# Four edits to a one-core adapter kernel: b2 of four batches by VectorE, a second W1 copy loaded four batches sooner, a ninth W1 by id, and a last store in halves

## Chip, core and metric

The kernel runs on one core of a Trainium2 chip. The metric is the device time of one execution in microseconds (us). Before the change the median of three runs is 308.9 us (308.59 to 309.42). The profiled execution took 308.95 us; its trace spans 307.2 us, so 1.75 us lie outside the span, and the TensorE clock granted over the span was 0.989 (1.00 in every stage up to 300 us).

## What is computed

There are 128 batches `b`, each a matrix `x[b]` of 128 rows by 512 columns in fp32, and each with an id `v = itok[b]` that picks one of 10 adapters:

```python
h = relu(x[b] @ W1[v] + b1[v])          # 512 -> 128
y = x[b] + h @ W2[v] + b2[v]            # 128 -> 512
n = (y - mean(y)) * rsqrt(var(y) + 1e-5)
out[b] = x[b] + n * gamma[v] + beta[v]
```

## The kernel before, in words

One batch is one tile of 128 partitions by 512 columns. One pass of the main loop (from L515, `i` from 3 to 129) moves the pipeline on by one batch: TensorE (PE) transposes batch `i` (four 128x128 transposes, L234), multiplies batch `i-1` by W1 (`down`, L257) and batch `i-2` by W2 (`up`, L274). ScalarE (ACT) copies the transposed batch out of PSUM (`copy_xT`, L238), applies bias and relu (L265), copies the W1 of a coming batch out of a resident table (`stage_w1`, L225) and squares with a sum (L310). VectorE (DVE) works on batch `b = i-3` and on the pair before: residual with its sum (L291), mean, the steps of the reciprocal root (L324, L326, L329), scaling by gamma (L353) and the final multiply-add (`finish`, L362). GpSimd (POOL) adds beta to x for every batch (L251) and b2 to x for most (L244). SyncE (SP) issues nearly all DMAs. Each engine's order is written by hand: `keep` ties each instruction behind the one before it on its engine, so an instruction that waits holds back everything behind it.

**b2** comes by one of three ways: POOL adds it to x ahead of time (`add_b2`); or PE adds it by a matmul of a one-column selector with the table rows, 96x512 in bf16, ahead of the W2 matmul (`b2_by_matmul`, L273); or DVE adds a row of the spread table `b2_b` to the result in PSUM (`vector_b2`, L284).

**W1** reaches a batch by three ways. Batches 0 to 7 get theirs from HBM by id (`load_first`, L154, 256 KB each, into a pool of five `w1s` buffers). From batch 8 on ACT copies it from a resident table. There are two tables: `w1e`, with rows grouped so that each partition holds four neighbouring rows of W1 (`load_early`, two DMAs of 1280 KB), for batches below EARLY = 24, whose transposes then read every fourth column of x; and `w1`, in the regular order, loaded in four quarters of 640 KB in runs of 512 bytes (`load_w1`, L103), for batches from 24 on. A quarter is a range of the reduction, not of the ids, so the first copy out of `w1` needs all four. FIRST = 8 is the first batch with a copy by ACT.

**SP's queue** around the change, in order: after the early loads come x of batches 12 to 15; the store of batches 0 and 1; x of 16 to 19; the stores of 2 and 3 and of 4 and 5; quarter 0 of `w1`; x of 20 to 23; the store of 6 and 7; quarter 1; the store of 8 and 9; quarter 2; x of 24 to 27; the store of 10 and 11; quarter 3. Each store (512 KB, L366) waits on SP for the DVE's `finish` of its second batch.

In ACT's order of pass `i` stand `copy_xT(i)`, `relu(i-1)`, `stage_w1(i+1)` and `square(i-3)`, from pass 11 on; PE has one PSUM buffer for the transposes, so those of batch `i+1` wait until `copy_xT(i)` has emptied it.

At the end (`tail`) the last five batches are finished one by one; the last one is scaled and finished over all 512 columns (L419) and stored by one DMA from SP (L415).

Of the kernel before, what the change touches and what calls it, by code (L numbers as in the profile page):

```python
# [16 lines left out]
P = 128  # L17
G = 4
EPS = 1e-5
FIRST = 8  # L20
EARLY = 24
LATE = 12
U = 2

# [2 lines left out]
def cond_resid_kernel(ctx: ExitStack, tc: tile.TileContext, x, itok, W1, b1, W2, b2, gamma, beta, out):  # L27
# [8 lines left out]
    nc = tc.nc  # L36
    B, S, H = x.shape
# [8 lines left out]
    def keep(ins):  # L46

        engine = ins.ins.engine
        if engine in last:
            tc.add_manual_dep(ins.ins, last[engine], behind, reason="kept order")  # L50
        last[engine] = ins.ins.name
        return ins
# [14 lines left out]
    E = B - 5  # L67
# [6 lines left out]
    def xb(b):  # L74
        return xs[b // G][:, b % G, :]
# [11 lines left out]
    def load_part(lo, hi):  # L87
        dst = xs[lo // G][:, lo % G : lo % G + hi - lo, :]
        keep(nc.sync.dma_start(out=dst, in_=x[lo:hi].rearrange("b s h -> s b h")))
# [11 lines left out]
    def load_w1(k):  # L101
        keep(
            nc.sync.dma_start(out=w1[:, :, k, :], in_=W1[:, k * P : (k + 1) * P, :].rearrange("l p a -> p l a"))  # L103
        )
# [28 lines left out]
    def lid(b, engine):  # L133
        g = b // G
        if (g, engine) not in lids:
            loads, vals = nc.values_load_multi_w_load_instructions(
                lang[0:1, g * G : (g + 1) * G],
                engines=[engine],
                min_val=0,
                max_val=L - 1,  # L140
                skip_runtime_bounds_check_because="clamped on the chip to 0..L-1 above",
            )
            for ins in loads:
                keep(ins)
            lids[g, engine] = vals
        return lids[g, engine][b % G]
# [4 lines left out]
    def load_first(b):  # L151
        w1s[b] = wp.tile([P, KC, A], FP, tag="w1s", name=f"w1s_{b}")
        src = W1[bass.ds(lid(b, ET.SP), 1)].rearrange("o (p k) a -> p (o k a)", k=KC)
        keep(nc.sync.dma_start(out=w1s[b].rearrange("p k a -> p (k a)"), in_=src))  # L154
# [5 lines left out]
    def load_early(lo, hi):  # L160
        dst = w1e[:, lo:hi].rearrange("p l k a -> p l (k a)")
        keep(nc.sync.dma_start(out=dst, in_=W1[lo:hi].rearrange("l (p k) a -> p l (k a)", k=KC)))
# [13 lines left out]
    xs[2] = xp.tile([P, G, H], FP, tag="x", name="x_2")  # L176
    load_part(2 * G, 2 * G + 2)
    load_early(0, 5)
    load_early(5, L)
    load_part(2 * G + 2, 3 * G)  # L180

    left = rp.tile([P, H], FP, tag="r", name="left")
# [29 lines left out]
    xT, hT, rs, os, ys, ssqs, nmeans, rstds = {}, {}, {}, {}, {}, {}, {}, {}  # L212
# [1 line left out]


    def b2_by_matmul(b):
        return b in (0, 1, 2, 3, 5, B - 1) or (b % 32 == 30 and b < E)

    def b2_by_vector(b):
        return 8 <= b < B - 8 and (b % 4 == 1 if b < 24 else b % 16 in (1, 6, 11))  # L220

    def stage_w1(b):
        w1s[b] = wp.tile([P, KC, A], FP, tag="w1s", name=f"w1s_{b}")
        src = (w1e if b < EARLY else w1).rearrange("p l k a -> p (l k a)")[:, bass.ds(lid(b, ET.Activation) * (KC * A), KC * A)]
        keep(nc.scalar.copy(w1s[b].rearrange("p k a -> p (k a)"), src))  # L225

    def transpose_x(b):
        pxs[b] = p_x.tile([P, KC, P], FP, tag="xT", name=f"pxT_{b}")
        for k in range(KC):
            if b < EARLY:  # L230
                cols = xb(b).rearrange("s (p k) -> s k p", k=KC)[:, k, :]
# [54 lines left out]
    def residual(b):  # L286
        r = rs.pop(b) if b in rs else xb(b)
        if b % 2 == 0:
            sums[b // 2] = st.tile([P, 2], FP, tag="sum", name=f"sum_{b // 2}")
        keep(  # L290
            nc.vector.scalar_tensor_tensor(ys[b], ys[b], 1.0, r, ALU.mult, ALU.add, accum_out=col(sums, b))  # L291
        )
# [45 lines left out]
    def deviation(g):  # L338
        root(ssqs[g], of_pair(g)[0])

    def rstd(g, n):
        t, u = of_pair(g)
        if n < 3:
            newton(n, ssqs[g], t, u)
        else:
            rstds[g] = st.tile([P, 2], FP, tag="rstd", name=f"rstd_{g}")
            newton_3(rstds[g], t, u)
            del ssqs[g], parts_of[g]
# [20 lines left out]
    def on(b):  # L369
        return 0 <= b < B  # L370
# [26 lines left out]
    def rstd_col(b):  # L397
        return rstds[b] if b > E else rstds[b // 2][:, b % 2 : b % 2 + 1]
# [12 lines left out]
        o = os[b // 2][:, b % 2, cols]  # L411
        keep(nc.gpsimd.tensor_tensor(o, n, o, ALU.add))

    def store_last(b, engine=nc.sync):
        keep(engine.dma_start(out=out[b], in_=os[b // 2][:, b % 2, :]))  # L415

    def finish_cols(b, cols=slice(0, H)):
        o = os[b // 2][:, b % 2, cols]
        keep(nc.vector.scalar_tensor_tensor(o, ys[b][:, cols], rstd_col(b), o, ALU.mult, ALU.add))  # L419

    def tail(b):
        p = E // 2
        residual(b)
        if b == E + 1:
            rstd(p, 1)
            scale(E - 1)
            rstd(p, 2)
            finish(E - 2)
            store(p - 1)
            rstd(p, 3)  # L430
            deviation_of(b)
            shift(E)
            by_pool(E, False)
        elif b == E + 2:
            rstd_of(b - 1, 1)
            negative_means(b // 2)
            rstd_of(b - 1, 2)
            finish_cols(E - 1)
            store_last(E - 1)
            rstd_of(b - 1, 3)  # L440
            store_last(E)
            deviation_of(b)
        elif b == E + 3:
            left, right = slice(0, H // 2), slice(H // 2, H)
            shift(b - 2)
            by_pool(b - 2, False)
            residual(b + 1)
            rstd_of(b - 1, 1)
            scale(b - 1)
            negative_means(b // 2)  # L450
            rstd_of(b - 1, 2)
            deviation_of(b)
            scale(b)
            rstd_of(b - 1, 3)
            rstd_of(b, 1)
            deviation_of(b + 1)
            rstd_of(b, 2)
            finish_cols(b - 1, right)
            by_pool(b - 1, True, left)
            store_last(b - 2, nc.scalar)  # L460
            store_last(b - 1, nc.scalar)
            rstd_of(b, 3)
            rstd_of(b + 1, 1)
            finish_cols(b)
            store_last(b)
            rstd_of(b + 1, 2)
            scale(b + 1)
            rstd_of(b + 1, 3)
            finish_cols(b + 1)
            store_last(b + 1)  # L470


    def spin(n, width):
# [41 lines left out]
    for i in range(3, B + U):  # L515
        b = i - U - 1
        if b > G and b % G == 2 and b // G + 3 < NG:
            load_x(b // G + 3)
        if i == 5:
            load_x(3)  # L520
        if i in (12, 14, 16, 18):
            load_w1((i - 12) // 2)
        if i == 4:
            up(2)
        if i == 5:
            up(3)
        if i > 3 and on(i):
            transpose_x(i)
        if b <= E:
            add_b2(b + 2)  # L530
            add_beta(b)
        if i > 4 and on(i - 1):
            down(i - 1)
        if i > 3 and on(i):
            copy_xT(i)
        if i > 4 and on(i - 1):
            relu(i - 1)
        if i + 1 >= LATE and on(i + 1):
            stage_w1(i + 1)
        if i > 5 and on(i - U):  # L540
            up(i - U)


        g, half = divmod(b, 2)
        p = g - 1
        mine, old = 0 <= p < B // 2, 0 <= p - 1 < B // 2
        if b == E:
            add_b2(b + 3)
            add_beta(b + 1)
            add_b2(b + 4)  # L550
            for n in range(b + 2, B):
                add_beta(n)
        if b > E:
            tail(b)
        elif half == 0:
            if on(b):
                vector_b2(b)
                residual(b)
            if mine:
                scale(2 * p)  # L560
                rstd(p, 1)
            if old:
                finish(2 * p - 1)
                store(p - 1)
        else:
            if on(b):
                vector_b2(b)
            if mine:
                rstd(p, 2)
            if on(b):  # L570
                residual(b)
            if mine:
                rstd(p, 3)
                scale(2 * p + 1)
            if on(b):
                negative_means(g)
            if mine:
                finish(2 * p)
        if 0 <= b <= E:
            square(b)  # L580
            if half == 1:
                deviation(g)
        if FIRST <= i + 1 < LATE:
            stage_w1(i + 1)

        for n, engine in ((i + 3, ET.Activation), (i - U + 3, ET.PE), (b + 1, ET.DVE), (b + 5, ET.Pool)):
            if on(n):
                lid(n, engine)
# [37 lines left out]
```

## Time and profile before

| what | number |
|---|---|
| median of three runs | 308.9 us |
| profiled execution, its own time | 308.95 us |
| its span | 307.2 us |
| PE busy | 296.1 us (96%) |
| DVE busy | 294.7 us (96%) |
| POOL busy | 284.4 us (93%) |
| ACT busy | 280.5 us (91%) |
| DMA | 77.59 MB, mean 253 GB/s |

A busy share says how long an engine had work in it, with overlapping instructions counted once. The timeline lists instructions in order: start, length, engine, line, operation, out<-in, and in brackets the idle time before it with what ended it. The view of stages gives the busy time of each engine, the granted clock, the share of the 16 DMA engines and the GB/s. For a DMA the timeline shows only the time of issuing it; its transfer and its landing (the moment at which its completion is signalled) are later, and are read from the answer for its line and from the trace's records of packets and landings.

### The profile page before, as it was taken

What the parts mean: (1) busy time and instruction counts of PE and PEld (TensorE: products, weight loads), DVE (VectorE), ACT (ScalarE), POOL (GpSimd) and SP (SyncE); (2) the same over time, 40 slices, a digit from 0 to 9 for tenths busy, and PEclk for the clock granted to TensorE, in tenths of its full rate; (3) what the DMA queues carried; (4) which work ended last, traced back from release to release, by engine and by line L of the source; (5) the groups of instructions that cost most, each with busy time, mean ns of one, the idle gap of its engine ahead of it and who ended that gap; (6) DMA issues with size and microseconds to landing.
All of it is one profiled execution on the core that took longest, in us unless ns stands there. A gap on an engine that the chain in (4) does not pass through costs nothing. (4 is left out here: it accounts for less than half of the span.)

```text
span 307.2 us, 6980 instructions
## 1 busy us (share of the span) xinstructions
PE 296.1 (96%) x1841; PEld 220.6 (72%) x1841; DVE 294.7 (96%) x825; ACT 280.5 (91%) x716; POOL 284.4 (93%) x238
## 2 busy tenths in 40 slices
PE   8999999999999999999999999999999999999970
PEld 3757778777777777777777777777777777777740
DVE  6877999999999999999999999999999999999994
ACT  3858999999999999999999999999999999999982
POOL 1349999998999999999999999999999999999994
PEclk9999999999999999999999999999999999999995
DMA  6999969986777667767876676777767666782244
GB/s 233 390 389 385 384 221 369 358 300 229 247 274 265 219 205 227 254 230 247 274 265 211 195 234 247 249 248 274 237 222 235 223 237 221 276 273 109 110 160 171
DMA packets 43481, 77.59 MB, mean 253 GB/s; under 512 B 1929, under 2 KB 7060, under 8 KB 43442
## 3 DMA queue, kind: packets, MB, share of 16 engines
q1 hardware_dynamic: 43094, 76.57, 72.2%
q10 hardware_dynamic: 348, 0.57, 0.5%
q8 instruction: 15, 0.25, 0.3%
q14 instruction: 24, 0.20, 0.2%
HBM read 43.58 MB, written 33.55 MB: 251 GB/s over the span
## 5 line engine op out<-in xcount | busy, mean ns | idle before, releaser
L251 POOL TENSOR_TENSOR o<-x,beta_b 128x512 f32<-128x512 f32 x128 | 163.4, 1289 | 9.5 <-DVE beta_b L210 9.5
L257 PE MATMUL ph<-xT,w1s 128*128 128x128 f32 x1024 | 135.3, 275 | 0.0
L244 POOL TENSOR_TENSOR r<-x,b_b 128x512 f32<-128x512 f32 x97 | 125.0, 1289 | 8.5 <-DVE b_b L210 6.2
L274 PE MATMUL py<-w,hT 128*128 x256 | 131.2, 594 | 0.0
L257 PEld LDWEIGHTS ph<-xT,w1s 128*128 128x128 f32 x1024 | 124.9, 192 | 1.0 <-ACT hT L265 0.5
L234 PEld LDWEIGHTS pxT<-ident,x 128*128 128x128 f32 x512 | 66.5, 152 | 66.0 <-issue 32.1
L353 DVE SCALAR_TENSOR_TENSOR py<-py,nmean,gamma_b 128x512 f32<-128x512 f32 x126 | 95.0, 754 | 0.0
L310 ACT ACTIVATE sq<-py,sum 128x512 f32<-128x512 f32 x124 | 86.3, 696 | 5.4 <-DVE nmean L298 2.4
L362 DVE SCALAR_TENSOR_TENSOR o<-py,rstd,o 128x512 f32<-128x512 f32 x122 | 90.9, 745 | 0.0
L234 PE MATMUL pxT<-ident,x 128*128 128x128 f32 x512 | 78.5, 276 | 0.0
L238 ACT COPY xT<-pxT 128x512 f32<-128x512 f32 x128 | 74.7, 584 | 3.9 <-PE pxT L234 3.9
L291 DVE SCALAR_TENSOR_TENSOR py<-py,r 128x512 f32<-128x512 f32 x97 | 67.1, 692 | 1.4 <-PE py L274 1.2
L225 ACT COPY w1s<-w 128x512 f32 x104 | 64.1, 616 | 0.0
L265 ACT ACTIVATE hT<-ph,b1T 128x128 f32<-128x128 f32 x128 | 47.3, 370 | 4.9 <-PE ph L257 2.5
L274 PEld LDWEIGHTS py<-w,hT 128*128 128x128 f32 x256 | 39.4, 192 | 1.8 <-issue 0.9
L310 ACT ACTIVATION_READ_ACCUMULATOR sq<-py,sum 128x1 f32 x124 | 25.4, 205 | 0.0
L291 DVE SCALAR_TENSOR_TENSOR py<-py,x 128x512 f32<-128x512 f32 x31 | 21.6, 698 | 1.6 <-issue 0.8
L320 ACT ACTIVATE root<-ssq,eps 128x2 f32<-128x2 f32 x62 | 16.5, 265 | 2.1
L284 DVE TENSOR_TENSOR py<-py,b_b 128x512 f32<-128x512 f32 x22 | 15.2, 691 | 0.1
L291 DVE DVE_READ_ACCUMULATOR py<-py,r 128x1 f32 x97 | 13.8, 142 | 0.0
L225 ACT COPY w1s<-w1e 128x512 f32 x16 | 9.8, 611 | 1.1 <-DMA w1e<-in_L_cond_W_dram 1.1
L324 DVE SCALAR_TENSOR_TENSOR part<-ssq,root 128x2 f32<-128x2 f32 x62 | 9.4, 151 | 0.9 <-ACT root L320 0.8
(54 smaller groups left out, 96.1 us busy)
## 6 DMA issues: line engine op xcount, KB each, us to landing
out_dram<-o SPq DMA_DIRECT2D x61, 512.0 KB, 3.3
x<-in_x_dram SPq DMA_DIRECT2D x29, 1024.0 KB, 6.4
x<-in_x_dram SPq DMA_DIRECT2D x6, 512.0 KB, 8.9
w1e<-in_L_cond_W_dram SPq DMA_DIRECT2D x2, 1280.0 KB, 11.7
w<-in_L_cond_W_dram SPq DMA_DIRECT2D x4, 640.0 KB, 7.4
w1s<-in_L_cond_W_dram SPq DMA_DIRECT2D x8, 256.0 KB, 8.2
w<-in_L_cond_W_dram SPq DMA_DIRECT2D x1, 1792.0 KB, 10.1
out_dram<-o SPq DMA_DIRECT2D x4, 256.0 KB, 2.0
```

The costliest lines, as they stand in the source:

```text
L225: keep(nc.scalar.copy(w1s[b].rearrange("p k a -> p (k a)"), src))
L234: keep(nc.tensor.transpose(pxs[b][:, k, :], cols, ident))
L238: keep(nc.scalar.copy(xT[b], pxs.pop(b)))
L244: keep(nc.gpsimd.tensor_tensor(rs[b], xb(b), b2_b[:, bass.ds(v * H, H)], ALU.add))
L251: keep(nc.gpsimd.tensor_tensor(os[g][:, j, :], xb(b), beta_b[:, bass.ds(v * H, H)], ALU.add))
L257: nc.tensor.matmul(phs[b], lhsT=w1s[b][:, k, :], rhs=xT[b][:, k, :], start=(k == 0), stop=(k == KC - 1))
L265: keep(nc.scalar.activation(hT[b], phs.pop(b), AF.Relu, bias=b1T[:, bass.ds(lid(b, ET.Activation), 1)]))
L274: keep(nc.tensor.matmul(ys[b], lhsT=hT[b], rhs=w2[:, bass.ds(v * H, H)], start=not m, stop=True))
L291: nc.vector.scalar_tensor_tensor(ys[b], ys[b], 1.0, r, ALU.mult, ALU.add, accum_out=col(sums, b))
L310: nc.scalar.activation(sq, ys[b], AF.Square, bias=col(sums, b), scale=-float(H), accum_out=col(ssqs, b))
L353: nc.vector.scalar_tensor_tensor(ys[b], ys[b], col(nmeans, b), gamma_b[:, bass.ds(v * H, H)], ALU.add, ALU.mult)
L362: nc.vector.scalar_tensor_tensor(o, ys.pop(b), rstds[g][:, j : j + 1], o, ALU.mult, ALU.add)
```

## The change

Four edits:

1. `b2` of batches 0 to 3 moves from the selector matmul on PE to an add on DVE.
2. The four quarters of `w1` are issued in passes 8, 10, 12 and 14 instead of 12, 14, 16 and 18, and `w1` is used from batch 16 on instead of 24.
3. Batch 8 also gets its W1 by id. Its load stands between the two halves of `load_early`, and the copy of batch 8 by ACT goes.
4. The last batch is finished and stored in two halves of 256 columns: the left one is issued by SP, the right one by ACT.

```diff
-FIRST = 8
-EARLY = 24
+FIRST = 9
+EARLY = 16
...
     load_early(0, 5)
+    load_first(2 * G)
     load_early(5, L)
...
     def b2_by_matmul(b):
-        return b in (0, 1, 2, 3, 5, B - 1) or (b % 32 == 30 and b < E)
+        return b in (5, B - 1) or (b % 32 == 30 and b < E)
 
     def b2_by_vector(b):
-        return 8 <= b < B - 8 and (b % 4 == 1 if b < 24 else b % 16 in (1, 6, 11))
+        return b < 4 or 8 <= b < B - 8 and (b % 4 == 1 if b < 24 else b % 16 in (1, 6, 11))
...
-    def store_last(b, engine=nc.sync):
-        keep(engine.dma_start(out=out[b], in_=os[b // 2][:, b % 2, :]))
+    def store_last(b, engine=nc.sync, cols=slice(0, H)):
+        keep(engine.dma_start(out=out[b][:, cols], in_=os[b // 2][:, b % 2, cols]))
...
-            finish_cols(b + 1)
-            store_last(b + 1)
+            for cols, engine in ((left, nc.sync), (right, nc.scalar)):
+                finish_cols(b + 1, cols)
+                store_last(b + 1, engine, cols)
...
-        if i in (12, 14, 16, 18):
-            load_w1((i - 12) // 2)
+        if i in (8, 10, 12, 14):
+            load_w1((i - 8) // 2)
```

## Prediction

> **What bounds the kernel.** The chain of waits explains only 2% of the span, so I read the stages first, then each engine's timeline. From 40 to 290 us PE, DVE and POOL are all busy for 99.9% of each stage. Which one sets the pace is seen in PE's timeline (start, length):
>
> ```profile
> 48.15 0.63 PE L234 MATMUL pxT<-ident,x 128*128 128x128 f32 x4
> 48.61 1.06 PE L257 MATMUL ph<-xT,w1s 128*128 128x128 f32 x8
> 49.50 1.02 PE L274 MATMUL py<-w,hT 128*128 x2
> 50.37 0.63 PE L234 MATMUL pxT<-ident,x 128*128 128x128 f32 x4
> ```
>
> These are the transposes of batch 16, `down` of 15, `up` of 14 and the transposes of 17. They follow each other at 0.46, 0.89 and 0.87 us, 2.22 us a pass; from batch 24 on, with regular transposes, at 0.44, 0.89 and 0.86, 2.19 a pass. After 35 us no pass is longer, but for 0.22 where a selector matmul stands. DVE's residual starts 0.04 to 1.03 us after the end of its batch's `up`, at batch 127 0.04 us: DVE is as loaded, but never further behind. So a hole in PE's stream is not made up later: a us lost there is a us at the end.
>
> **ACT is the way in.** Its timeline, at the copy of batch 16 (the ninth L225, since the first, at 31.29, is batch 8's):
>
> ```profile
> 47.79 0.61 ACT L225 COPY w1s<-w1e 128x512 f32 x1
> 48.30 0.70 ACT L310 ACTIVATE sq<-py,sum 128x512 f32<-128x512 f32 x1
> 48.88 0.20 ACT L310 ACTIVATION_READ_ACCUMULATOR sq<-py,sum 128x1 f32 x1
> 48.97 0.59 ACT L238 COPY xT<-pxT 128x512 f32<-128x512 f32 x1
> ```
>
> Behind the copy stand the square of batch 12 and `copy_xT(16)`, for which PE's transposes of 17 wait (one PSUM buffer). After a late start of that copy, PE goes on 1.18 + 0.59 + 0.05 (hand-over, as at 32.40 to 32.45) = 1.8 us later. What such a wait looks like is there already once, on the first table:
>
> ```profile
> 31.29 0.62 ACT L225 COPY w1s<-w1e 128x512 f32 x1 [1.05 <-DMA w1e<-in_L_cond_W_dram]
> ```
>
> **The DMAs.** SP's issues, and the DMA share by stage (last two columns: share of the 16 engines, GB/s):
>
> ```profile
> 39.87 1.31 SPq L103 DMA_DIRECT2D w<-in_L_cond_W_dram  x1
> 41.28 0.76 SPq L71 DMA_DIRECT2D x<-in_x_dram  x1
> 44.39 0.38 SPq L366 DMA_DIRECT2D out_dram<-o  x1
> 44.83 0.46 SPq L103 DMA_DIRECT2D w<-in_L_cond_W_dram  x1
> ```
> ```profile
> 34.00:38.00 4.00, 4.00 (x26) 2.94 (x26) 3.58 (x12) 3.97 (x12) 4.00 (x4) 1.00 1.04 400
> 38.00:40.00 2.00, 2.00 (x15) 1.53 (x14) 1.94 (x6) 2.00 (x5) 2.00 (x2) 1.00 0.18 68
> 42.00:46.00 4.00, 4.00 (x26) 3.06 (x26) 4.00 (x13) 3.96 (x11) 4.00 (x4) 1.00 0.88 270
> 46.00:50.00 4.00, 4.00 (x29) 3.29 (x28) 4.00 (x12) 3.83 (x12) 4.00 (x5) 1.00 1.06 378
> ```
>
> The engines are full until the early loads have drained (38.2 us by the packet records), have a dip of 2 us, and are full again when the quarters of `w1` come. Before, the last quarter is issued at 53.76, lands at 62.7, and is first read at 65.6: 3 us to spare.
>
> ```profile
> DMA to landing us min/median/max: 6.3/7.4/8.9
> ```
>
> That is the answer for L103: three of the four quarters have a landing, and none took under 6.3 us.
>
> **Part 2, W1 sooner: the price.** Quarter 3 now stands behind the store of 6 and 7 in pass 14. That store was issued at 44.39; with about 1.1 us of gain at the start (below) it goes at 43.3, and quarter 3 at 43.7. Its reader, ACT's copy of batch 16 in pass 15, would come at 47.79 - 1.1 = 46.7. The lead has shrunk from 11.8 us to 3.0, under half the shortest landing. When does it land? I take the engines as serving SP's DMAs in order, as the landings of before suggest: x of 20 to 23, issued 1.4 us after quarter 0, landed at 47.8, after its 46.2; quarter 2 (55.3) ahead of x of 24 to 27 (57.4), issued right behind it. Bytes ahead: before, everything up to the store of 2 and 3 had drained at 38.2. Added are W1 of batch 8 (256 KB at 390 GB/s, 0.7) and quarters 0 and 1, which now come before that point. A quarter's packets of 512 bytes go at 284 GB/s (43 to 44 us, where nothing else moved), 2.3 us each. So 38.2 + 0.7 + 4.6 = 43.5 with no dip. Then the store of 4 and 5 (512 KB, 1.35), quarter 2 (2.3), x of 20 to 23 (1 MB, 2.7), the store of 6 and 7 (1.35) and quarter 3 (2.3): 53.5. From the last packet to the landing the four quarters took 0.8 to 1.7, mean 1.1: **54.6**. The copy of 16 waits 54.6 - 46.7 = 7.9 us on ACT; behind it the square, `copy_xT(16)`, then all of PE from the transposes of 17 on. Those come at 54.6 + 1.8 = 56.4 instead of 50.37: **+6.0**. Bounds for the landing: 50.0 if it takes the shortest landing of a quarter (43.7 + 6.3), 57.3 if it takes that of x of 12 to 15 in the storm of early loads, 13.6. That makes +1.4 and +8.7; I take 54.6, since the queue ahead is counted from bytes.
>
> The Trainium skill, "DMA: Bandwidth & Descriptors", section "Queues, rings and completion order", says that SP's DMAs share one row of rings, and that each engine consumes a ring in order: this speaks against the change, since a load issued sooner into a full queue doesn't overtake. The landings above agree. The same page's fit for one DMA, 2.0 us plus bytes over 436e3 (section "Anatomy of one DMA", made on GpSimd's path), would give an estimate of 3.5 us, a landing at 47.2 and the second rival's time below; no quarter here was that quick.
>
> Its gain: seven passes from batch 17 to 23 with regular transposes, 2.22 to 2.19: **-0.2**. Earlier ones lie before the wait.
>
> **Part 1, b2 on DVE.** PE loses four matmuls at 0.22 us (20.09 to 20.32):
>
> ```profile
> 20.09 0.38 PE L273 MATMUL py<-parts,pick 96*128 96x512 bf16 x1
> 20.32 1.02 PE L274 MATMUL py<-w,hT 128*128 x2
> ```
>
> -0.9 on PE up to batch 5. DVE gains four adds of 0.70 and 0.03 of hand-over (48.41 to 49.13 at L284), 2.9 us, and between 19.5 and 27.91 it has 0.84 + 0.33 + 0.82 + 0.85 = 2.8 us idle: they fill it, and the residual of batch 4 stays at 27.9. Without that idle time they would cost up to 2.9. From there DVE runs at its own 2.07 a batch (a pair from 42.28 to 46.42) instead of at PE's, and reaches batch 8 at 36.2 instead of 37.31: -1.1 on both engines.
>
> **Part 3, a ninth W1 by id.** Its buffer is free when `down(3)` ends (17.0); SP gets there at 16.6, so SP waits 0.4 and has a register load and 0.4 of issue, and behind it stand the second half of `w1e` and x of 10 and 11, all in a queue ten us long: they land 0.7 later, `w1e` at 31.9, x of 10 at 33.3. ACT no longer needs `w1e` at 30.2 but at about 32.5, so its 1.05 us wait goes, and with it 0.15 + 0.11 + 0.04 in PE's passes of 9 to 11: -0.3. POOL, idle 0.69 for x of 10 now, idles 1.4, and leads DVE by 4 us or more all the way: nothing.
>
> All of parts 1 and 3 comes before 50 us, and the wait of part 2 ends by bytes, not by when ACT arrives: it swallows them. **0.**
>
> **Part 4, halves.** A half costs DVE 0.40 to its successor (300.42 to 300.82 at L419), so the left store leaves 0.3 sooner, the right ends 0.1 later and has ACT's issue (0.38) behind that of batch 125 (to 303.6). But from 303 to 305.5 the DMA engines are full with the four last stores: their bytes end when they ended. 0, within -0.3 and +0.3.
>
> **Sum**, against the execution's own 308.95 (the median, 308.9, is as good as equal): +6.0 - 0.2 + 0 = **314.8**. Bounds: +1.4 - 0.2 gives 310.2, +8.7 - 0.2 gives 317.5.
>
> **Rivals.** (a) *The queue is shorter than its bytes* (DMAs overtake, or the dip is used better): the landing is at 50.0 to 52, time 310.2 to 312.2. For it: the 6.3 us of quarter 0. Against: that one was issued into the dip, which is gone. (b) *No wait*: quarter 3 lands by 47.4, where 47.4 + 1.8 meets PE's transposes of 17 at 50.37 - 1.1 = 49.2; from there on parts 1 and 3 count. DVE's 1.1 is the smaller gain and sets it: 307.8. For it: only that SP issues the quarter 3 us ahead. Against: a landing of 3.7 us, where 6.3 is the least seen. (c) *The move of the quarters does not take effect*: each stays behind a store's wait for DVE; but these waits are of passes 7, 9, 11 and 13, so the issues do come 9 us sooner, at 30.0, 34.2, 38.8 and 43.7. It falls.
>
> **Chances**: forecast (312.3 to 317.5) 0.77; (a) 0.12; above 317.5 0.03; within 0.3% (what a measurement of this kernel can tell from no change) 0.02; (b) 0.06. So slower 0.92, same 0.02, faster 0.06; the range 310.2 to 317.5 holds 0.89.
>
> **What would show it.** On ACT, one idle stretch of some 8 us ahead of the first copy out of `w1`, ended by a DMA, near 46.7 to 54.6; one hole of 6 to 7 us in PE before the transposes of 17; the DMA share near 1 from 38 to 54 with no dip; before the hole, `up(4)` 0.9 sooner, the residual of 4 at 27.9, no wait at the copy of batch 9; after it 2.19 a pass. Wrong if the hole is missing (then rival b, and my reading of the queue falls), or if ACT waits at batch 9 too.

## The result and the profile after

The changed kernel takes 316.5 us (median of six runs, 315.97 to 317.83) against 309.15 us before. The ratio, an estimate from all runs and not the quotient of the two medians, is 1.0246 with a 95% interval of 1.0224 to 1.0267. The profiled execution took 316.37 us, with a span of 314.6 us: 7.4 us more than the one before. The forecast was 314.8 us, in a range of 310.2 to 317.5.

ACT's timeline of the kernel after, at the copies of batches 15 and 16:

```profile
44.41 0.61 ACT L226 COPY w1s<-w1e 128x512 f32 x1
...
46.41 0.37 ACT L266 ACTIVATE hT<-ph,b1T 128x128 f32<-128x128 f32 x1
54.30 0.62 ACT L226 COPY w1s<-w 128x512 f32 x1 [7.52 <-DMA w<-in_L_cond_W_dram]
54.83 0.68 ACT L311 ACTIVATE sq<-py,sum 128x512 f32<-128x512 f32 x1
55.41 0.19 ACT L311 ACTIVATION_READ_ACCUMULATOR sq<-py,sum 128x1 f32 x1
55.50 0.57 ACT L239 COPY xT<-pxT 128x512 f32<-128x512 f32 x1
```

The first copy out of `w1` waits 7.52 us for a DMA; it had been ready at 46.8. The square and the copy of the transposed batch 16 stand behind it, as the prediction said. What PE's timeline of the kernel after shows at this place:

```profile
47.03 0.60 PE L235 MATMUL pxT<-ident,x 128*128 128x128 f32 x4
47.46 1.06 PE L258 MATMUL ph<-xT,w1s 128*128 128x128 f32 x8
48.36 1.02 PE L275 MATMUL py<-w,hT 128*128 x2
56.13 1.11 PE L235 MATMUL pxT<-ident,x 128*128 128x128 f32 x4 [6.75 <-ACT xT L239]
57.03 1.92 PE L258 MATMUL ph<-xT,w1s 128*128 128x128 f32 x8
58.74 1.53 PE L275 MATMUL py<-w,hT 128*128 x2
60.10 0.60 PE L235 MATMUL pxT<-ident,x 128*128 128x128 f32 x4
```

The hole is where it was forecast: the transposes of batch 17 come at 56.13 instead of 50.37. But look at the pass behind the hole. `down` takes 1.92 instead of 1.06, and the next transposes come 3.97 us later, where a pass takes 2.19. Stages of the kernel after (last three columns: granted clock, DMA share, GB/s):

```profile
38.00:40.00 2.00, 2.00 (x15) 1.61 (x14) 1.94 (x7) 1.84 (x6) 2.00 (x3) 1.00 1.05 385
...
49.00:50.00 1.00, 0.38 (x1) 0.00 (x0) 1.00 (x3) 0.00 (x0) 1.00 (x2) 1.00 1.05 397
52.00:53.00 1.00, 0.00 (x0) 0.00 (x0) 0.00 (x0) 0.00 (x0) 0.51 (x1) 0.96 1.14 371
53.00:54.00 1.00, 0.00 (x0) 0.00 (x0) 0.00 (x0) 0.00 (x0) 1.00 (x2) 0.50 1.06 402
57.00:58.00 1.00, 1.00 (x7) 1.00 (x6) 0.14 (x2) 0.97 (x4) 0.00 (x0) 0.50 0.06 25
59.00:60.00 1.00, 1.00 (x2) 0.30 (x2) 0.00 (x0) 1.00 (x3) 0.00 (x0) 0.63 0.37 145
60.00:61.00 1.00, 1.00 (x10) 0.89 (x9) 0.62 (x3) 0.80 (x3) 0.00 (x0) 1.00 0.97 377
```

Two things can be seen. The dip in the DMA share at 38 to 40 us (0.18 before) is gone: 1.05. And the TensorE clock, 1.00 while PE works, falls to 0.50 at 52.9, when PE has been without work for 3.5 us, and is whole again at 59.75, 3.6 us after PE took up work.

**Where the 7.4 us are**, from the starts of the transposes in both traces, batch by batch:

| up to | after minus before | what |
|---|---|---|
| batches 11 to 16 | -1.12 | parts 1 and 3, but for 0.46 that is there at batches 1 to 3 already |
| batch 17 | +5.76 | the hole, which swallows the 1.12 |
| batch 18 | +7.52 | the pass at half clock, +1.76 |
| batches 24 to 88 | +7.35 | regular transposes of 17 to 23, -0.17 |
| end of the span | +7.4 | 0.15 more between batches 88 and 96, 0.1 less at the end |

The 0.46 us at batches 1 to 3 is no work of the change: none of the four edits reaches that far forward. The start differs from one profiled execution to the next. Against the profile before, the transposes of batch 1 come between 0.70 us sooner and 0.13 us later in the other twelve profiles, and 0.64 sooner in `halves_alone`, where only the last batch was edited.

So the theory to test: all of the loss is the wait for the last quarter of `w1`, a hole of 6.75 us in PE, and a halved clock behind it. Its rivals: that the adds on DVE or the ninth load cost time too; that the long pass is the pipeline filling up again, not the clock; that the quarter is late for another reason than the bytes ahead of it.

### The profile page after: what moved, and what is told of

The parts are those of the page before. It is cut to its first block, busy times and chain, and to the rows that moved or that the text cites. A ratio compares the mean times of both kernels' runs of the same rounds, so it can differ in the third digit from the quotient of the medians.

```text
span 314.6 us, 6978 instructions
## 1 busy us (share of the span) xinstructions
PE 296.4 (94%) x1837; PEld 220.5 (70%) x1837; DVE 297.5 (95%) x830; ACT 279.9 (89%) x715; POOL 284.3 (90%) x238
## 5 line engine op out<-in xcount | busy, mean ns | idle before, releaser
L245 POOL TENSOR_TENSOR r<-x,b_b 128x512 f32<-128x512 f32 x97 | 123.7, 1275 | 15.8 <-DVE b_b L211 6.2
L235 PEld LDWEIGHTS pxT<-ident,x 128*128 128x128 f32 x512 | 65.6, 149 | 74.3 <-ACT xT L239 37.4
L226 ACT COPY w1s<-w 128x512 f32 x112 | 69.0, 616 | 7.5 <-DMA w<-in_L_cond_W_dram 7.5
L285 DVE TENSOR_TENSOR py<-py,b_b 128x512 f32<-128x512 f32 x26 | 18.1, 698 | 0.8 <-PE py L275 0.6
L299 DVE SCALAR_TENSOR_TENSOR nmean<-sum,py 128x2 f32<-128x2 f32 x64 | 10.2, 159 | 0.1
```

The costliest lines, as they stand in the source:

```text
L235: keep(nc.tensor.transpose(pxs[b][:, k, :], cols, ident))
L245: keep(nc.gpsimd.tensor_tensor(rs[b], xb(b), b2_b[:, bass.ds(v * H, H)], ALU.add))
```

## Experiments

Each ratio is against the kernel before, run on the same chip; its median there was 309.0 to 309.14 us.

| run | median us | ratio, 95% interval |
|---|---|---|
| `no_early_w1` | 308.06 | 0.9967 (0.9950 to 0.9985) |
| `early_w1_alone` | 316.58 | 1.0251 (1.0235 to 1.0266) |
| `w1_from_20` | 308.68 | 0.9989 (0.9980 to 0.9999) |
| `pe_kept_busy` | 315.24 | 1.0203 (1.0187 to 1.0219) |
| `b2_alone` | 309.17 | 0.9989 (0.9965 to 1.0013) |
| `ninth_alone` | 308.42 | 0.9979 (0.9961 to 0.9996) |
| `halves_alone` | 309.0 | 0.9994 (0.9980 to 1.0008) |
| `w1_from_18` | 312.3 | 1.0089 (1.0067 to 1.0111) |
| `w1_by_act_queue` | 316.18 | 1.0228 (1.0191 to 1.0265) |
| `x20_behind_w1` | 314.47 | 1.0165 (1.0124 to 1.0206) |
| `w1_from_18_busy` | 310.68 | 1.0050 (1.0034 to 1.0066) |

### Which part costs: `no_early_w1` and `early_w1_alone`

```diff
# no_early_w1, from the kernel after
-EARLY = 16
+EARLY = 24
...
-        if i in (8, 10, 12, 14):
-            load_w1((i - 8) // 2)
+        if i in (12, 14, 16, 18):
+            load_w1((i - 12) // 2)
```

> The changed kernel with part 2 undone (quarters in passes 12 to 18, second table from batch 24); parts 1, 3 and 4 stay. Theory: the whole loss is the wait for quarter 3 and what it does to TensorE's clock, and parts 1 and 3 gain 1.1 us that the wait swallowed. Then 308.0 us against 309.15 (ratio 0.996), no idle time on ACT before a copy of W1, no hole in PE. Rival: the four adds on VectorE and the ninth load cost time themselves: 309.2 or more.

Measured: 308.06 us, 0.94 less than before, with no wait for `w1` and no such hole. The other three parts together gain. (PE's lead over the kernel before shrinks from 1.25 to 0.89 us at batches 20 and 21; why stays open.)

`early_w1_alone` is the reverse edit, made in the kernel before.

> The kernel before with part 2 alone. Theory: the wait ends when quarter 3 lands, not when ACT arrives; without the ninth load (256 KB, 0.7 us of transfer) ahead of it it lands at about 53.6 instead of 54.25, and ACT arrives 1.1 us later, so ACT waits about 5.7 us instead of 7.5 and the time is 315.8 us. Rival: parts 1 and 3 have a share in the loss: 314.5 or less.

Measured: 316.58 us, as slow as all four parts together. ACT's timeline of this kernel:

```profile
53.84 0.62 ACT L225 COPY w1s<-w 128x512 f32 x1 [6.17 <-DMA w<-in_L_cond_W_dram]
```

The copy starts at 53.84 (53.6 expected) after a wait of 6.17 us (5.7 expected). Part 2 alone is the loss; that parts 1 and 3 bring ACT there a us sooner changes only how long it waits. The profiled execution took 315.54 us, 0.3 under the forecast of 315.8. The other three took 316.55 to 316.93, at a mean clock of 0.980 to 0.982 where the profiled one has 0.985, so more of the halved clock is likely in them; they have no trace that would show it.

### Is it when the quarters are used, or that they are moved: `w1_from_20`

```diff
-EARLY = 16
+EARLY = 20
```

> The changed kernel with the second table used from batch 20 instead of 16, the quarters issued in the same early passes. Theory: quarter 3 lands at 54.3 as before, ACT comes to the copy of batch 20 at about 55.5, so nobody waits: 307.9 us (1.1 from the start and 4 regular transposes, 0.1). Rival: issuing the quarters into the full queue costs by itself, through x and stores that land later: 309 or more.

Measured: 308.68 us. ACT's timeline of this kernel, at the first copy out of `w1`:

```profile
55.72 0.62 ACT L226 COPY w1s<-w 128x512 f32 x1
```

ACT copies batch 20 with no wait and there is no hole: four batches decide between 316.5 and 308.7. But the gain is 0.3, not 1.1. PE's transposes are 0.84 to 1.06 us ahead of before from batch 11 to batch 127; the end is not. POOL's timeline of this kernel, in the queue's busiest time and at the end:

```profile
53.09 1.28 POOL L252 TENSOR_TENSOR o<-x,beta_b 128x512 f32<-128x512 f32 x1 [1.06 <-DMA out_dram<-o]
```
```profile
294.62 2.56 POOL L252 TENSOR_TENSOR o<-x,beta_b 128x512 f32<-128x512 f32 x2
297.07 1.33 POOL L411 TENSOR_TENSOR n<-n,gamma_b 128x512 f32<-128x512 f32 x1
```

A store that lands late holds back POOL by 1.06 us (its output buffer is not free); in `no_early_w1` POOL has no such wait. From 53 us on POOL has no gap up to its multiply for batch 123, the first of its steps at the end. This starts at 297.07, only 0.20 sooner than before (297.27). In `no_early_w1` it starts at 296.59, 0.68 sooner. The chain of work that ended last runs through POOL from 265 us to the end here, and through DVE's last steps in `no_early_w1`. So the rival had a point: the moved loads cost 0.6 us of the gain (308.68 against 308.06), through POOL.

### Clock or filling up: `pe_kept_busy`

```diff
-        ys[b] = p_y.tile([P, H], FP, tag="y", name=f"py_{b}")
+        if b not in ys:
+            ys[b] = p_y.tile([P, H], FP, tag="y", name=f"py_{b}")
...
+    def fill(b, n):
+        ys[b] = p_y.tile([P, H], FP, tag="y", name=f"py_{b}")
+        for _ in range(n):
+            keep(nc.tensor.matmul(ys[b], lhsT=ones, rhs=ones[:, 0:1].to_broadcast([P, H]), start=True, stop=True))
...
+        if i == 17:
+            fill(i - U, 26)
```

> The changed kernel with 26 idle matmuls (96x512-like, 0.22 us each, into the PSUM buffer that the next result overwrites) put into PE's hole ahead of the transposes of batch 17. ACT's wait stays 7.5 us. Theory: the 1.8 us that the first pass after the hole takes too long (4.0 instead of 2.2) is the halved clock from 52.9 to 59.8; with PE busy the clock stays whole, the pass takes 2.2 and the time is 314.7 us. Rival: the long pass is the pipeline filling up again behind ACT: 316.5 us, with the clock whole.

PE's timeline of this kernel:

```profile
50.80 5.82 PE L489 MATMUL py<-ones 128*128 128x512 bf16 x26 [0.85 <-DVE o L364]
56.71 0.66 PE L235 MATMUL pxT<-ident,x 128*128 128x128 f32 x4
57.20 1.06 PE L258 MATMUL ph<-xT,w1s 128*128 128x128 f32 x8
58.09 1.02 PE L276 MATMUL py<-w,hT 128*128 x2
58.98 0.65 PE L235 MATMUL pxT<-ident,x 128*128 128x128 f32 x4
```

Measured: 315.24 us, 1.3 less than the changed kernel (1.1 by the two profiled executions). ACT waits the same 7.5 us, but the pass after the hole takes 2.27 us instead of 3.97 (from 56.71 to 58.98) and the clock is 1.00 to the end of PE's work. It is the clock. (The gain is smaller than 1.8 since in this profile quarter 3 is there 0.6 us later: the copy starts at 54.88 instead of 54.30.)

### How short a hole still costs the clock: `w1_from_18` and `w1_from_18_busy`

The first is the kernel after with `EARLY = 18`.

> The changed kernel with the second table used from batch 18. ACT reaches that copy at about 51.3 us, quarter 3 is there at 54.3 to 54.8, so ACT waits 3 to 3.4 us and TensorE has a hole of some 2.5 us, shorter than the 3.5 us after which the clock was halved in the changed kernel. Theory: the clock stays whole, the pass after the hole takes 2.2 us and the time is 309.0 - 0.9 + 2.5 - 0.1 = 310.5 us. Rival: each hole costs the 1.8 us of the long pass too: 312.2 us.

Measured: 312.3 us. That is the rival's number, and the theory's step, a whole clock, was wrong. PE's timeline of this kernel, and its stages (last three columns: granted clock, DMA share, GB/s):

```profile
52.70 1.02 PE L275 MATMUL py<-w,hT 128*128 x2
56.62 1.12 PE L235 MATMUL pxT<-ident,x 128*128 128x128 f32 x4 [2.89 <-ACT xT L239]
57.52 1.91 PE L258 MATMUL ph<-xT,w1s 128*128 128x128 f32 x8
59.23 1.92 PE L275 MATMUL py<-w,hT 128*128 x2
```
```profile
55.00:56.00 1.00, 0.00 (x0) 0.00 (x0) 0.00 (x0) 1.00 (x4) 1.00 (x2) 0.95 1.07 416
60.00:62.00 2.00, 2.00 (x7) 1.29 (x6) 0.82 (x3) 1.03 (x3) 2.00 (x3) 0.50 0.89 274
62.00:63.00 1.00, 1.00 (x7) 1.00 (x7) 1.00 (x4) 0.59 (x1) 0.85 (x1) 0.63 0.84 193
```

The hole is only 2.9 us, yet the clock is halved, from 55.9 (2.2 us after PE's last work) to 62.7 (6.1 us after PE began again). That costs 3.0 us in the two passes behind the hole, as much as the hole itself. This profile is of the slowest of the ten runs (313.69), and not every run is like it: two took 309.99 and 310.49 us, at a mean clock of 0.989 and 0.990 as in the kernel before; the other eight took 311.98 to 313.69, at 0.978 to 0.987. The second kernel puts six idle matmuls into this hole (`fill(i - U, 6)` at `i == 19`).

> The kernel with the second table from batch 18, with 6 idle matmuls in TensorE's hole ahead of the transposes of batch 19 (they can start only when a PSUM buffer is free, some 1.2 us into the hole). Theory: of that kernel's 312.3 us some 1.8 are the clock, halved after a hole of 2.9 us; with no stretch of more than some 1.2 us without a matmul the clock stays whole in every run: 310.5 us, with runs within 0.5 us of each other instead of 3.7. Rival: 312.3, spread as before.

PE's timeline of this kernel:

```profile
54.35 1.46 PE L489 MATMUL py<-ones 128*128 128x512 bf16 x5 [0.55 <-DVE o L364]
56.55 0.66 PE L235 MATMUL pxT<-ident,x 128*128 128x128 f32 x4 [0.73 <-ACT xT L239]
```

The trace holds five of the six idle matmuls. Measured: 310.68 us, ten runs from 310.13 to 311.40, a mean clock of 0.988 to 0.990 in all ten; in the profile the clock is 1.00 to the end of PE's work, and ACT's wait is 3.33 us where it was 3.47. Its own forecast holds: with about the same wait but no halved clock the kernel takes 1.6 us less, and no run is above 311.4, though the spread of 1.3 us is wider than the 0.5 forecast.

### Why the quarter is late: `x20_behind_w1` and `w1_by_act_queue`

```diff
# x20_behind_w1, from the kernel after
-        if b > G and b % G == 2 and b // G + 3 < NG:
+        if b > G and b % G == 2 and b // G + 3 < NG and i != 13:
...
             load_w1((i - 8) // 2)
+        if i == 14:
+            load_x(5)
```

> The changed kernel with the load of x of batches 20 to 23 (1 MB) issued behind quarter 3 instead of ahead of it; nothing else moves. Theory: quarter 3 lands 2.7 us sooner, the time that 1 MB takes, at 51.5; ACT waits 4.8 us instead of 7.5, TensorE's hole is 3.1 instead of 5.8, the clock is halved all the same: 313.8 us. Rival: the transfers mix in the engines and the order in the queue counts little: 315.5 or more.

ACT's timeline of this kernel:

```profile
51.72 0.62 ACT L226 COPY w1s<-w 128x512 f32 x1 [4.90 <-DMA w<-in_L_cond_W_dram]
```

The copy starts at 51.72, 2.6 us sooner, for a forecast of 2.7; ACT waits 4.90 us, forecast 4.8. By the packet records the last packet of `w1` ends at 51.24 here and at 53.94 in the kernel after. The order in SP's queue counts as the prediction had it. The time, 314.47, is 0.7 above the forecast; the clock is halved from 51.7 to 58.5 in the profile, 5.0 us of it with PE at work, where the kernel after has 3.6.

```diff
# w1_by_act_queue, from the kernel after, in load_w1
-            nc.sync.dma_start(out=w1[:, :, k, :], ...
+            nc.scalar.dma_start(out=w1[:, :, k, :], ...
```

> The changed kernel with the four quarters issued by ACT in the same passes, so that they stand in ACT's queue and not behind x and the stores in SP's. Theory: quarter 3 is late because SP's DMAs are served in order; in a queue of its own it shares the engines with SP's from its issue at about 43 us on and lands at 48 to 50 instead of 54; ACT pays some 0.5 us for each issue; ACT waits 1 to 2 us, TensorE has a hole of 1 us or less, the time is 309.5 to 311. Rival: the bytes of all queues are served alike, so it lands near 54 and the time is 316.

Measured: 316.18 us, the rival's number. ACT's timeline of this kernel, then the answer for L103:

```profile
41.53 0.38 ACTq L103 DMA_DIRECT2D w<-in_L_cond_W_dram  x1
41.95 0.59 ACT L239 COPY xT<-pxT 128x512 f32<-128x512 f32 x1 [2.89 <-DMA w<-in_L_cond_W_dram]
...
54.18 0.62 ACT L226 COPY w1s<-w 128x512 f32 x1 [4.92 <-DMA out_dram<-o]
```
```profile
DMA to landing us min/median/max: 10.8/12.0/13.3
```

In a queue of its own a quarter takes longer to land: 10.8 to 13.3 us for the three whose landing the trace lists, against 6.3 to 8.9 before. The last one is there no sooner: issued at 44.82, its last packet ends at 53.65, and the copy starts at 54.18 (54.30 in the kernel after). (The trace names a store as what ended that wait, but the copy reads `w1` alone, and the time fits the quarter.) Besides, ACT is held up 2.89 us at the third issue. By the packet records the two queues share the engines by packets, not by bytes: from 34 to 36 us 316 packets of 512 bytes went beside 298 of 2048. So the separate queue with the short runs got a fifth of the bytes. The theory is thus right for SP's own queue and did not carry over to a second one: the engines are as full as in the kernel after (a DMA share of 1.08 from 34 to 40 us, 1.05 there from 38 to 40), so how much has to be moved by then decides here too.

### The other three parts by themselves

> The kernel before with part 1 alone: b2 of batches 0 to 3 by VectorE. Theory: TensorE loses four selector matmuls (0.9 us) and VectorE's adds fill its idle time; ACT still waits for w1e at the copy of batch 8, now for longer (it gets there sooner), so part of the gain is lost there: 308.4 us, -0.6. Rival: the adds push VectorE behind and the gain is nothing: 309.0.

`b2_alone` (only the two functions of b2 changed): 309.17 us, no gain. ACT's timeline:

```profile
31.08 0.62 ACT L225 COPY w1s<-w1e 128x512 f32 x1 [1.71 <-DMA w1e<-in_L_cond_W_dram]
```

PE is 1.03 us ahead at the transposes of batch 8 (0.68 of it already at batches 2 and 3, ahead of the edit) and 0.22 ahead at those of 9: ACT comes sooner and waits 1.71 for `w1e` instead of 1.05. So the wait for `w1e` swallows the gain as long as part 3 does not take it away. Another 0.4 us are lost at 55.5 us, where DVE idles before the residual of batch 16; what it waited for the trace does not tell.

> The kernel before with part 3 alone: W1 of batch 8 by id. Theory: ACT's 1.05 us wait for w1e goes and with it 0.3 us of TensorE's passes 9 to 11; x of batches 10 and 11 lands 0.7 us later, which only GpSimd meets, and it has room: 308.7 us, -0.3. Rival: the load ahead of w1e and x costs as much as it saves: 309.0 or more, with GpSimd late at the end.

`ninth_alone` (FIRST = 9 and the added `load_first`): 308.42 us, -0.7. In the profile, of a run of 308.62 us, the gain on PE is 0.24 from batch 11 on, about the 0.3 forecast. Half of the runs are at 307.9 to 308.2, the rest at 308.6 and above, and why is open. What part 1 adds to this (308.06 in `no_early_w1`) is not clear of the noise: the intervals overlap.

> The kernel before with part 4 alone: the last batch finished and stored in halves from two queues. Theory: the four last stores fill the DMA engines from 302.5 to 305.5 us, so their bytes end when they did: 309.0 us, 0 within 0.2. Rival: the left half leaves 0.3 us sooner and the last transfer is half as long: 308.6.

`halves_alone` (only `store_last` and the last two lines of `tail`): 309.0 us against 309.14, nothing that can be told from no change, as the theory had it.

## Why the prediction was right, and where it was short

- **What bounds**: right. A hole of x us in PE was x us at the end: +7.35 at batch 24, +7.35 at batch 88. (POOL is not busy for 99.9% of every stage, as the prediction says, but for 93% from 60 to 80 us, 18.64 of 20; nothing hangs on it here.)
- **Part 2, who waits**: right to the instruction. ACT was ready for the copy of 16 at 46.8 (46.7 forecast); behind the copy PE went on 1.83 us later (1.8).
- **Part 2, when it lands**: right within half a us. The wait ended at 54.30, 54.6 forecast from bytes. `x20_behind_w1` confirms the count: 1 MB less ahead, 2.6 us sooner. The bounds of 50.0 and 57.3 were not needed. That it is as close as 0.3 us is in part luck, since two terms were off against each other: the last packet ended at 53.94 (53.5 forecast) and the landing came 0.3 later (1.1 forecast). In the trace before, too, quarter 0 lands 0.4 us and quarter 3 0.8 us after its last packet, where the prediction has 0.8 to 1.7 for the four; and by their last completion signals x of 20 to 23, quarter 2 and x of 24 to 27 land at 49.0, 55.5 and 58.4, where the prediction reads 47.8, 55.3 and 57.4. The order that it drew from them stands. Nor did the quarters go out as forecast (at 30.0, 34.2, 38.8 and 43.7) but at 30.14, 35.98, 40.23 and 45.48, as SP's issues ahead of them took up to 3.2 us each; the sum counts bytes and did not use these times.
- **The size of the loss**: short by 1.6 us in the profiled execution (316.37 against 314.8). The step that failed is "after it 2.19 a pass". The first pass after the hole took 3.97, since the clock had been halved; `pe_kept_busy` shows it. The sum was +6.0 and should have been +6.0 and half of the time that PE works before its clock is back, 3.62 us here. The signs were in the profile of before: its last stage, with PE out of work, has a granted clock of 0.53.
- **Regular transposes**: -0.17, forecast -0.2.
- **Part 1**: right on the path, the residual of batch 4 at 27.60 (27.9 forecast) and that of batch 8 1.11 sooner (1.1). That the number fits so well is luck: 0.46 of it came from an earlier start, which no edit made. That it was worth nothing here is right too (`early_w1_alone` is as slow as the whole change). That part 1 hangs on part 3 was not said.
- **Part 3**: right: no wait at the copy of batch 9, which comes at 32.21 (32.5). "POOL: nothing" holds only because of the hole; in `w1_from_20`, without it, POOL's lost time is what limits the gain to 0.3.
- **Part 4**: right, 0.
- **Rivals**: (a) is refuted by the landing, (b) by the wait. Its price without a wait, 307.8, is nearly met by `no_early_w1` (308.06) and missed by `w1_from_20` (308.68) for POOL's sake. `no_early_w1` beats both kernels: parts 1, 3 and 4 with `w1` left as it was.

## What to carry to other kernels

A load that is issued earlier into a full queue lands when the bytes ahead of it are through: count them from the last moment at which the queue was empty, and compare that with the first reader's time, not the issue. Price a hole in TensorE with its clock: besides its own length, half of the time that the work behind it runs before the clock is whole. Where two edits lie ahead of one wait, the wait swallows what they gain, so measure them with the wait taken away.

## What the hardware showed

The clock does not fall after a fixed time without work, nor come back after a fixed time with it. In the five profiles with a halved clock at a hole it fell 2.2 to 5.0 us after PE's last matmul and was whole 3.0 to 6.1 us after PE began again, and each half-rate stretch lasted 3.41 or 6.83 us. The Trainium skill, "TensorE: Matmul & The Clock Gate", section "Part 1: The HAM clock gate", tells of a window of 3.4 us that runs on freely; the lengths here agree, one and two such windows. Its advice to leave no idle gaps over about 3 us (section "Why this matters for your kernels") leaves too little room here: a hole of 2.9 us cost the clock in the profile of `w1_from_18`, and eight of its ten runs lie 1.5 us or more above the other two.

The traces also show when the clock changes. In all thirteen profiles every stretch between two changes is a whole multiple of 3.413 us, counted from the first rise: 47.79 is 14 such steps, 51.20 is 15, 249.17 is 73 and 296.96 is 87. At the five falls at a hole PE had worked for 0 to 1.23 us of the step just past (1.16 in `x20_behind_w1`, 1.23 in `w1_from_18`, nothing in the other three). At the five recoveries it had worked for 3.0 us of the step (`early_w1_alone`) up to all of it; 2.7 us in `w1_from_18`, from 56.62 to 59.33, did not bring the clock back, and so its half-rate stretch lasted two steps. As far as these five holes show, then, what a short hole costs hangs on where it falls in the steps. That this also parts the ten runs of `w1_from_18` is likely, but only one of them has a trace.
